# Two attention layers in float32: transposing the softmax maxima of two head groups at once

## The chip, the cores and the metric

The kernel runs on one core of a Trainium2 chip. The metric is device time in microseconds of one launch. The core has a matrix engine (TensorE, PE in the profile, its weight loads PEld), a vector engine (DVE), a scalar engine (ACT), GpSimd (POOL) and a queue for transfers (SP). Matrix products land in PSUM, which has eight banks of 128 x 512 float32.

## What is computed

Two transformer blocks act on x of 4 batches x 512 tokens x 256 channels, all float32. Each has cross attention to a context of 512 tokens (16 heads of 16 channels) and a feed-forward part. The first feed-forward has ternary weights, the second picks one of four experts per token.

```python
x = x + tanh(g_xattn[0]) * xattn0(layernorm(x), ctx, ctx)   # 16 heads, bias -0.1*|q-k|
x = x + tanh(g_ffn[0])   * ffn0(layernorm(x))               # 256 -> 1024 -> 256, ternary
x = x + tanh(g_xattn[1]) * xattn1(layernorm(x), ctx, ctx)   # 16 heads, relu'd q, k, v
x = x + tanh(g_ffn[1])   * ffn1(layernorm(x))               # 4 experts, top 1, then layernorm

# each attention, per batch and head
scores = q @ k.T / 4 (+ bias)
attn   = softmax(scores, axis=-1)
out    = attn @ v
```

## The kernel before

**Groups.** The heads of one batch in one layer are cut into four groups of four heads. Two groups share a chunk of 128 channels (`tt`), one takes the even heads (`e` = 0) and the other the odd (`e` = 1). A head has 16 channels but a slot of 32 rows: in `qs` and `ks` the rows of the other half are zero, and they are spare. There are 2 x 4 x 4 = 32 groups, in the order of `groups`.

**Softmax without a second pass.** A group is worked in two stages. `maxima` (L496) makes scores with queries in the rows, for 128 queries at a time, and DVE takes each row's maximum (L508) into `m_sb`. `shifted` (L559) transposes the four tiles of maxima (L565, PE) into a bank and subtracts that bank from the queries (L567, DVE), which puts the maximum, negated, into a spare row that meets a row of ones in the keys. Layer 0 carries the distance bias in eight more spare rows in the same way. `weights` (L512) then makes scores with keys in the rows from the shifted queries `q2s`, ACT takes the exponential (L523), in layer 0 POOL multiplies the diagonal tile (L526), and `weighted` (L544, PE line L551) multiplies with the values. The last column of the values is one, so the sum comes with it; `divided` (L596) or `divided_blocks` (L577) divides.

**Units.** A unit is one tile of 128 rows of one group; there are 128. `scores(u, vs)` (L531) emits the weights of unit u and the maxima of a later unit side by side: a quad is two products of each kind, in four row tiles of 32 rows, each into a bank of its own. A unit normally has two quads. The four maxima of a unit are drained by DVE, the four weight products by ACT. All PSUM tiles come from one rotation of eight banks, so a product waits until the tile eight places earlier has been read.

**Lead.** Maxima run `LEAD` = 6 units ahead of the weights; four units stand before the first weights, and units 0 and 1 take two units of maxima each:

```python
vs = [u + NT] if u < 0 else [2 * u + NT, 2 * u + NT + 1] if u < LEAD - NT else [u + LEAD]
```

**Slots.** After the scores of unit u, `slot(u)` (L1092) emits everything else: at u % 4 == 0 the values product of the group before, at u % 4 == 2 the transposes of the next group and a division. The rest comes from chains: lists of steps, each with a PE cost and a gap in units to the step before it, and each chain with a start and an end in units. A planner takes the step that is due first while the slot's cost is under `SLOT` = 3.1. Chains hold the layernorms (`prepare`), the key and query projections (`project`, two per batch and layer, one for each chunk), the values, the first feed-forward (`ffn0`), the routing and the first expert tiles. The engines execute in the order in which the program emits. After unit 127 the rest of the expert tiles follows in an order written out by hand.

**Names in the profile.** `pm` is a bank of maxima scores, `psc` of weight scores, `pmT` of transposed maxima, `po` of the values product, `pn` of a transposed output, `pk`, `pq`, `pva` of projections, `ph` and `py_f` of the first feed-forward, `pg` of an expert's hidden layer.

Of the kernel before, what the change touches and what calls it, by code (L numbers as in the profile page):

```python
# [19 lines left out]
P = 128  # L20
# [4 lines left out]
HG = 4  # L25
# [12 lines left out]
T_AHEAD = 4  # L38
LEAD = 6
SLOT = 3.1  # L40

# [7 lines left out]
def flamingo_kernel(ctx: ExitStack, tc: tile.TileContext, t: dict, out: bass.AP):  # L49
# [11 lines left out]
    def bank_psum(name):  # L61
        return ps.tile([P, 512], F32, tag="bank", name=name)
# [71 lines left out]

    kpos = act.tile([P, S], F32, tag="q2", name="kpos")
    nc.gpsimd.iota(
# [4 lines left out]

    def query_key_biases():
        for i in range(2):
            for e in range(2):
                nc.vector.tensor_scalar_mul(bqk[:, i, :, e], qkb[:, i, :], half[:, e : e + 1])
# [17 lines left out]
    )  # L163
    m_sb = [[], []]

    def maxima_places(layer):
        for e in range(2):
            m = act.tile([P, NT, HG, HP], F32, tag=f"m{layer}{e}", name=f"m{layer}{e}", bufs=1)
            nc.gpsimd.memset(m, 0.0)
            if layer == 0:  # L170
                for n in range(NT):
                    r = SPARE[e] + 1 + n
                    nc.gpsimd.memset(m[:, n, :, r : r + 1], -1.0)
                    nc.gpsimd.tensor_copy(
                        m[:, n, :, r + NT : r + NT + 1],
                        tok[:, n : n + 1].unsqueeze(1).to_broadcast([P, HG, 1]),
                    )
            m_sb[layer].append(m)

# [264 lines left out]
    def project(layer, b, tt):  # L444
# [12 lines left out]
        def key_half(pk, e):  # L457
            k = act.tile([P, S], F32, tag="k", name=f"k{nm}{e}", bufs=5)
            h = half[:, e : e + 1]
            if layer == 0:  # L460
                nc.vector.scalar_tensor_tensor(k, pk, h, kext[tt, e], ALU.mult, ALU.add)
            elif e == 0:
                nc.scalar.activation(k, pk, AF.Relu, bias=kone[:, e : e + 1], scale=h)
            else:
                nc.vector.tensor_scalar(k, pk, h, kone[:, e : e + 1], ALU.mult, ALU.max)
            ks[layer, b, tt, e] = k
# [29 lines left out]
    def maxima(v, pair):  # L496

        g = groups[v // NT]
        n = v % NT
        pm = [bank_psum(f"pm{v}{pair}{i}") for i in range(2)]  # L500
        for i in range(2):
            score(pm[i], qs[g], ks[g], 2 * pair + i, n)
        m = m_sb[g[0]][g[3]]
        r = SPARE[g[3]]

        def drain():
            for i in range(2):
                nc.vector.tensor_reduce(m[:, n, 2 * pair + i, r : r + 1], pm[i], AX.X, ALU.max)  # L508

        return drain  # L510
# [47 lines left out]

    def shifted(s):  # L559

        g = groups[s]
        m = m_sb[g[0]][g[3]]
        pm = bank_psum(f"pmT{s}")
        for n in range(NT):
            nc.tensor.transpose(pm[:, ts(n, P)], m[:, n].rearrange("p h w -> p (h w)"), ident)  # L565
        q2s[g] = act.tile([P, S], F32, tag="q2", name=f"q2_{s}")
        nc.vector.tensor_tensor(q2s[g], qs[g], pm, ALU.subtract)  # L567

# [460 lines left out]
    def first_unit(layer, b):  # L1029
        return 4 * NT * (B * layer + b)  # L1030

    ffn = head = None
    ffns = []
    for b in range(B):
        first, rest = ffn0(b)
        end = first_unit(1, b) - 15
        head = chain(first, 4 * NT * (b + 1) + 3, 4 * NT * (b + 1) + 9, head)
        ffn = chain(rest, 0, end, head, ffn)
        ffns.append(ffn)
    for layer in range(2):  # L1040
        for b in range(B):
            u0 = first_unit(layer, b)
            lead, values = prepare(layer, b)
            if (layer, b) == (0, 1):
                *early, early_rows, turn_1 = (job for job, *_ in lead)
                (early_values, *_), later_values = values
                turned_1 = chain([later_values, (turn_1, 0.9, 1)], 1, 4)
                chain(project(layer, b, 0), 5, u0 - LEAD - 2, turned_1)
            elif u0:
                chain(  # L1050
                    [*lead, *project(layer, b, 0)], u0 - 14, u0 - LEAD - 2,
                    ffns[b] if layer else None,
                )
                chain(values, u0 - 8, u0 + 2)
            chain(project(layer, b, 1), max(u0 - 4, 0), u0)
    (totals1, *_), *quant1 = quantize(w1f, "w1")
# [35 lines left out]
    def slot(u):  # L1092
# [4 lines left out]
        if u % NT == 2 and u > 0:  # L1097
            s = u // NT
            if s + 1 < len(groups):
                shifted(s + 1)  # L1100
                used += 0.5
# [24 lines left out]

    maxima_places(0)
    value_places(0)
# [14 lines left out]
    for u in range(-NT, n_units):  # L1143
        if u == 0:
            shifted(0)
            early_values()
            other_constants()
        if u == 4:
            maxima_places(1)
        if u == first_unit(0, B - 1) + 1:  # L1150
            attn_w.append(load_attn(1))
        if u == first_unit(1, 2) + 2:

            wo1 = [const.tile([P, NF // 2, D], F32, tag=f"cT{i}", name=f"wo1{i}") for i in range(2)]
            for i, w in enumerate(wo1):
                rw = t["wo1"][i * FF // 2 : (i + 1) * FF // 2, :]
                nc.sync.dma_start(out=w, in_=rw.rearrange("(c p) f -> p c f", p=P))
        vs = [u + NT] if u < 0 else [2 * u + NT, 2 * u + NT + 1] if u < LEAD - NT else [u + LEAD]
        scores(u, [v for v in vs if v < n_units])
        if u < -NT + 2:  # L1160
# [189 lines left out]
```

## Time and profile before

| | |
|---|---|
| median of 3 runs | 851.79 us (850.83 to 853.1) |
| profiled execution | 852.66 us, its span 851.0 us |
| first score quad of a weight unit | 29.9 us |
| start of the last unit | 699.2 us |
| PE, DVE, ACT, POOL busy | 96%, 66%, 50%, 33% |
| maxima, L508 | 512 instructions, 316.7 us of DVE |
| exponentials, L523 | 512 instructions, 267.0 us of ACT |
| transposes of maxima, L565 | 128 instructions, 21.1 us of PE |
| subtraction, L567 | 32 instructions, 21.6 us of DVE |

In the profile a float32 product counts as two instructions on PE, a transpose as one. "Busy" is the union of the times of a group's instructions, and "idle before" is how long the engine had nothing to do before them, with the engine and line that released it. An instruction on PE is listed when it starts, and its end is modelled. A bank that is not yet free delays the product that wants it.

### The profile page before, as it was taken

How to read it: one execution, taken by the hardware profiler on the slowest of the kernel's cores; microseconds unless marked ns; L12 is line 12 of the kernel's file. 1: busy time of each engine (PE TensorE's matmuls, PEld its weight loads, DVE VectorE, ACT ScalarE, POOL GpSimd, SP SyncE). 2: the span in 40 equal slices, each digit the busy share in tenths (PEclk: the TensorE clock that was granted, in tenths of full speed). 3: DMA queues.
4: the chain of work that ended last, by engine and by line, in shares of the span. 5: the costliest groups of instructions: out<-in, count | busy, mean ns of one | idle time of the engine just before them, and what ended most of it. 6: DMA issues, size and time to landing. Idle time of an engine off the chain costs nothing. (4 is left out here: it accounts for less than half of the span.)

```text
span 851.0 us, 13599 instructions
## 1 busy us (share of the span) xinstructions
PE 818.3 (96%) x5241; PEld 460.4 (54%) x5241; DVE 561.3 (66%) x1218; ACT 422.5 (50%) x886; POOL 277.8 (33%) x446
## 2 busy tenths in 40 slices
PE   6999999999999999999999999999999999999994
PEld 3444444435464346444464445544445567889993
DVE  6868778766856785668746775577786655863343
ACT  2575565653554462556426563357555666224331
POOL 4636455524242433321101120003013224354542
PEclk9999999999999999999999999999999999999998
DMA  9100000000000000000000010001004424536540
GB/s 318 62 1 1 1 1 2 1 1 1 1 13 26 1 1 1 25 2 1 1 2 25 0 50 1 1 1 35 17 13 147 164 70 148 188 108 239 190 152 15
DMA packets 18096, 43.07 MB, mean 51 GB/s; under 512 B 2222, under 2 KB 12208, under 8 KB 15600
## 3 DMA queue, kind: packets, MB, share of 16 engines
q0 software_dynamic: 5488, 28.13, 9.8%
q1 hardware_dynamic: 12128, 13.54, 4.6%
q8 instruction: 41, 0.67, 0.3%
q10 hardware_dynamic: 416, 0.54, 0.2%
q14 instruction: 23, 0.19, 0.1%
HBM read 35.91 MB, written 6.68 MB: 50 GB/s over the span
## 5 line engine op out<-in xcount | busy, mean ns | idle before, releaser
L508 DVE TENSOR_REDUCE m<-pm 128x1 f32<-128x512 f32 x512 | 316.7, 681 | 107.8 <-PE psc L494 105.3
L523 ACT ACTIVATE p<-psc 128x512 f32<-128x512 f32 x512 | 267.0, 602 | 151.2 <-PE psc L494 149.0
L494 PE MATMUL psc<-q,k 32*128 32x512 f32 x1024 | 278.6, 622 | 0.2 <-DVE h L672 0.2
L494 PE MATMUL pm<-k,q 32*128 32x512 f32 x1024 | 262.0, 615 | 1.3 <-ACT q L481 0.9
L526 POOL TENSOR_TENSOR p<-p,dec 128x256 f32<-128x256 f32 x128 | 93.6, 735 | 177.2 <-ACT p L523 177.2
L494 PEld LDWEIGHTS pm<-k,q 32*128 32x128 f32 x1024 | 92.7, 184 | 83.5 <-issue 50.0
L494 PEld LDWEIGHTS psc<-q,k 32*128 32x128 f32 x1024 | 106.4, 183 | 51.7 <-issue 25.7
L551 PE MATMUL po<-p,v 128*32 128x512 f32 x1024 | 116.5, 595 | 1.9 <-DVE m L508 1.9
L551 PEld LDWEIGHTS po<-p,v 128*32 128x32 f32 x1024 | 31.7, 109 | 81.8 <-issue 60.8
L996 PE MATMUL pg<-xs,wg 128*128 128x128 f32 x608 | 72.1, 276 | 0.9 <-DVE m L508 0.9
L996 PEld LDWEIGHTS pg<-xs,wg 128*128 128x128 f32 x608 | 70.4, 192 | 4.4 <-DVE m L508 1.9
L1178 PE MATMUL pyf<-wo,ha 128*128 128x256 f32 x304 | 68.4, 379 | 0.0
L619 POOL TENSOR_TENSOR x<-x,o 128x256 f32<-128x256 f32 x14 | 10.2, 728 | 174.3 <-DVE o L612 131.7
L1009 ACT ACTIVATE ha<-pg,wg 128x128 f32<-128x128 f32 x120 | 34.2, 368 | 62.4 <-PE pg L996 57.0
L1178 PEld LDWEIGHTS pyf<-wo,ha 128*128 128x128 f32 x304 | 56.4, 190 | 7.0
L664 PE MATMUL ph<-xTf,w1q 128*128 128x512 f32 x128 | 60.0, 605 | 0.0
L557 ACT COPY oT<-po 128x512 f32<-128x512 f32 x32 | 18.7, 584 | 77.6 <-PE po L551 77.6
L379 PE MATMUL py_f<-w2q,h 128*128 128x256 f32 x256 | 57.2, 381 | 0.0
L379 PEld LDWEIGHTS py_f<-w2q,h 128*128 128x128 f32 x256 | 48.0, 190 | 9.4 <-DVE m L508 3.0
L451 PE MATMUL pk<-cT,wk 128*128 128x512 f32 x68 | 35.3, 644 | 7.3 <-DMA cT<-in_ctxT_dram 7.3
L664 PEld LDWEIGHTS ph<-xTf,w1q 128*128 128x128 f32 x128 | 22.6, 189 | 30.4 <-issue 18.2
L1182 DVE TENSOR_TENSOR y<-y,pyf 128x256 f32<-128x256 f32 x19 | 8.0, 421 | 43.3 <-PE pyf L1178 39.1
(223 smaller groups left out, 811.2 us busy)
## 6 DMA issues: line engine op xcount, KB each, us to landing
x<-in_x_dram SPq DMA_DIRECT2D x4, 512.0 KB, 7.0
rows_d<-xn_f SPq DMA_DIRECT2D x4, 512.0 KB, 3.0
rows_d<-x SPq DMA_DIRECT2D x4, 512.0 KB, 3.1
cT<-in_ctxT_dram SPq DMA_DIRECT2D x3, 512.0 KB, 9.6
w1q<-in_w_dram SPq DMA_DIRECT2D x1, 1024.0 KB
w2q<-in_w_dram SPq DMA_DIRECT2D x1, 1024.0 KB, 11.3
wo<-in_wo_dram SPq DMA_DIRECT2D x2, 512.0 KB
rows<-in_rows_dram SPq DMA_DIRECT2D x1, 640.0 KB, 9.3
```

The lines of the kernel that those rows point to most:

```text
L379: nc.tensor.matmul(py[:, n, :], lhsT=operand(c, n0 + n), rhs=w[:, c, :], start=(c == 0), stop=(c == chunks - 1),)
L451: nc.tensor.matmul(pp, lhsT=attn_w[layer][w][:, c, ts(tt, P)], rhs=src[:, c, :], start=(c == 0), stop=(c == NC - 1),)
L494: nc.tensor.matmul(out_, lhsT=lhs[r, ts(n, P)], rhs=rhs[r, :], start=True, stop=True)
L508: nc.vector.tensor_reduce(m[:, n, 2 * pair + i, r : r + 1], pm[i], AX.X, ALU.max)
L523: nc.scalar.activation(p[:, i, :], psc[i], AF.Exp, scale=SCALE)
L526: nc.gpsimd.tensor_tensor(d, d, dec.unsqueeze(1).to_broadcast([P, 2, P]), ALU.mult)
L551: nc.tensor.matmul(po[i * HP : (i + 1) * HP, :], lhsT=v_sb[b % 2][0][:, kt, c0 : c0 + HP], rhs=ps_exp[NT * s + kt, i // 2][:, i % 2, :], s ...
L557: nc.scalar.copy(pos[s], po)
L664: nc.tensor.matmul(ph, lhsT=w1q[:, c, ts(f, P)], rhs=st["xT"][:, c, :], start=(c == 0), stop=(c == NC - 1),)
L996: nc.tensor.matmul(ph[:, f, :], lhsT=w[:, c, ts(f2 * NF // 2 + f, P)], rhs=xs[j][:, c, :], start=(c == 0), stop=(c == NC - 1),)
L1009: nc.scalar.activation(ha[:, f, :], (ha if src is None else src)[:, f, :], AF.Gelu, bias=biases[j][:, fa : fa + 1],)
L1178: nc.tensor.matmul(py, lhsT=hs[j, f // 4][:, f % 4, :], rhs=wo1[f // 4][:, f % 4, :], start=(f == 0), stop=(f == NF - 1),)
```

## The change

The first ten groups stay single. From the tenth on the two groups of a chunk, which share their 128 rows, are one turn. Both write their maxima into the same tile: the even group's into row 16 of each head's 32, the odd group's into row 0. One set of four transposes then serves both, and each group takes from it only its own spare rows: the subtraction becomes a multiplication of the bank with a column that is -1 in the group's spare rows and 0 elsewhere, plus the queries. Since the maxima of both groups have to be there, maxima lead the weights by ten units: units 24, 28, 32 and 36 get a second unit of maxima (a third quad). There are two tiles for maxima that alternate between turns, in place of four, and both have the bias rows; POOL clears those rows after the last two turns of layer 0. Keys get one buffer more and shifted queries one. The projections and layernorms of a chunk are due by the unit in which its maxima are emitted, so their chains start and end earlier.

```diff
--- before.py
+++ after.py
@@ -37,6 +37,8 @@
 T_LIST = T_ALL - LISTS[-1][1]
 T_AHEAD = 4
 LEAD = 6
+MORE = (24, 28, 32, 36)
+PAIRED = 10
 SLOT = 3.1
 
 
@@ -132,7 +134,7 @@
 
 
 
-    kpos = act.tile([P, S], F32, tag="q2", name="kpos")
+    kpos = act.tile([P, S], F32, tag="q2", name="kpos", bufs=3)
     nc.gpsimd.iota(
         kpos, pattern=[[1, S]], base=0, channel_multiplier=0, allow_small_or_imprecise_dtypes=True
     )
@@ -140,6 +142,7 @@
     kext = {}
 
     def query_key_biases():
+        nc.vector.tensor_scalar(spare, half, -1.0, None, ALU.add)
         for i in range(2):
             for e in range(2):
                 nc.vector.tensor_scalar_mul(bqk[:, i, :, e], qkb[:, i, :], half[:, e : e + 1])
@@ -161,21 +164,22 @@
     nc.gpsimd.iota(
         tok, pattern=[[-P, NT]], base=0, channel_multiplier=-1, allow_small_or_imprecise_dtypes=True
     )
-    m_sb = [[], []]
-
-    def maxima_places(layer):
-        for e in range(2):
-            m = act.tile([P, NT, HG, HP], F32, tag=f"m{layer}{e}", name=f"m{layer}{e}", bufs=1)
+    m_sb = []
+    spare = const.tile([P, 2], F32, tag="spare", name="spare")
+
+    def maxima_places():
+
+        for i in range(2):
+            m = act.tile([P, NT, HG, HP], F32, tag=f"m{i}", name=f"m{i}", bufs=1)
             nc.gpsimd.memset(m, 0.0)
-            if layer == 0:
-                for n in range(NT):
-                    r = SPARE[e] + 1 + n
-                    nc.gpsimd.memset(m[:, n, :, r : r + 1], -1.0)
-                    nc.gpsimd.tensor_copy(
-                        m[:, n, :, r + NT : r + NT + 1],
-                        tok[:, n : n + 1].unsqueeze(1).to_broadcast([P, HG, 1]),
-                    )
-            m_sb[layer].append(m)
+            for n in range(NT):
+                rows_of = m[:, n].rearrange("p h (e w) -> p (h e) w", e=2)
+                nc.gpsimd.memset(rows_of[:, :, 1 + n : 2 + n], -1.0)
+                nc.gpsimd.tensor_copy(
+                    rows_of[:, :, 1 + NT + n : 2 + NT + n],
+                    tok[:, n : n + 1].unsqueeze(1).to_broadcast([P, 2 * HG, 1]),
+                )
+            m_sb.append(m)
 
     def counting(shape, pattern, base, up, name):
 
@@ -455,7 +459,7 @@
             return pp
 
         def key_half(pk, e):
-            k = act.tile([P, S], F32, tag="k", name=f"k{nm}{e}", bufs=5)
+            k = act.tile([P, S], F32, tag="k", name=f"k{nm}{e}", bufs=6)
             h = half[:, e : e + 1]
             if layer == 0:
                 nc.vector.scalar_tensor_tensor(k, pk, h, kext[tt, e], ALU.mult, ALU.add)
@@ -500,7 +504,7 @@
         pm = [bank_psum(f"pm{v}{pair}{i}") for i in range(2)]
         for i in range(2):
             score(pm[i], qs[g], ks[g], 2 * pair + i, n)
-        m = m_sb[g[0]][g[3]]
+        m = m_sb[turn_of[v // NT] % 2]
         r = SPARE[g[3]]
 
         def drain():
@@ -556,15 +560,30 @@
         pos[s] = act.tile([P, S], F32, tag="oT", name=f"oT{s}")
         nc.scalar.copy(pos[s], po)
 
-    def shifted(s):
-
-        g = groups[s]
-        m = m_sb[g[0]][g[3]]
-        pm = bank_psum(f"pmT{s}")
+
+    turns = [(s,) for s in range(PAIRED)]
+    turns += [(s, s + 1) for s in range(PAIRED, len(groups), 2)]
+    turn_of = {s: i for i, of in enumerate(turns) for s in of}
+
+    def shifted(i):
+
+        m = m_sb[i % 2]
+        pm = bank_psum(f"pmT{i}")
         for n in range(NT):
             nc.tensor.transpose(pm[:, ts(n, P)], m[:, n].rearrange("p h w -> p (h w)"), ident)
-        q2s[g] = act.tile([P, S], F32, tag="q2", name=f"q2_{s}")
-        nc.vector.tensor_tensor(q2s[g], qs[g], pm, ALU.subtract)
+        for s in turns[i]:
+            g = groups[s]
+            q2s[g] = act.tile([P, S], F32, tag="q2", name=f"q2_{s}", bufs=3)
+            nc.vector.scalar_tensor_tensor(
+                q2s[g], pm, spare[:, g[3] : g[3] + 1], qs[g], ALU.mult, ALU.add
+            )
+        if i in last_turns:
+
+            rows_of = m.rearrange("p n h (e w) -> p (n h e) w", e=2)
+            nc.gpsimd.memset(rows_of[:, :, 1 : 1 + 2 * NT], 0.0)
+
+    last_turn = turn_of[len(groups) // 2 - 1]
+    last_turns = (last_turn - 1, last_turn)
 
 
 
@@ -1029,30 +1048,43 @@
     def first_unit(layer, b):
         return 4 * NT * (B * layer + b)
 
+
+    units_of, phase_of = {}, {}
+    for u in range(-NT, n_units):
+        many = 2 if 0 <= u < LEAD - NT or u in MORE else 1
+        units_of[u] = range(len(phase_of), min(len(phase_of) + many, n_units))
+        phase_of |= {v: u for v in units_of[u]}
+    for i, of in enumerate(turns):
+
+        assert phase_of[NT * of[-1] + NT - 1] < NT * of[0] - 2 or i == 0
+        assert i + 2 >= len(turns) or phase_of[NT * turns[i + 2][0]] >= NT * of[0] - 1
+
     ffn = head = None
     ffns = []
     for b in range(B):
         first, rest = ffn0(b)
-        end = first_unit(1, b) - 15
+        end = phase_of[first_unit(1, b)] - 9
         head = chain(first, 4 * NT * (b + 1) + 3, 4 * NT * (b + 1) + 9, head)
         ffn = chain(rest, 0, end, head, ffn)
         ffns.append(ffn)
     for layer in range(2):
         for b in range(B):
             u0 = first_unit(layer, b)
+            at = [phase_of[u0 + 2 * NT * i] for i in range(2)]
             lead, values = prepare(layer, b)
             if (layer, b) == (0, 1):
                 *early, early_rows, turn_1 = (job for job, *_ in lead)
                 (early_values, *_), later_values = values
                 turned_1 = chain([later_values, (turn_1, 0.9, 1)], 1, 4)
-                chain(project(layer, b, 0), 5, u0 - LEAD - 2, turned_1)
+                chain(project(layer, b, 0), 5, at[0] - 2, turned_1)
             elif u0:
                 chain(
-                    [*lead, *project(layer, b, 0)], u0 - 14, u0 - LEAD - 2,
+                    [*lead, *project(layer, b, 0)], at[0] - 8, at[0] - 2,
                     ffns[b] if layer else None,
                 )
                 chain(values, u0 - 8, u0 + 2)
-            chain(project(layer, b, 1), max(u0 - 4, 0), u0)
+            soon = 4 if (layer, b) == (1, B - 1) else 6
+            chain(project(layer, b, 1), max(at[1] - soon, 0), at[1] - 2)
     (totals1, *_), *quant1 = quantize(w1f, "w1")
     (totals2, *_), *quant2 = quantize(w2f, "w2")
     totals = {0: (totals1, 0), 1: (totals1, 2), 2: (totals2, 0), 3: (totals2, 2)}
@@ -1096,8 +1128,8 @@
             used += 3.5
         if u % NT == 2 and u > 0:
             s = u // NT
-            if s + 1 < len(groups):
-                shifted(s + 1)
+            if s + 1 < len(groups) and turns[turn_of[s + 1]][0] == s + 1:
+                shifted(turn_of[s + 1])
                 used += 0.5
             if s > 0 and not by_blocks(s - 1):
                 divided(s - 1)
@@ -1124,7 +1156,7 @@
             if c["steps"]:
                 c["ready"] = u + c["steps"][0][0][2]
 
-    maxima_places(0)
+    maxima_places()
     value_places(0)
     query_key_biases()
     lead, values = prepare(0, 0, nc.vector, lambda: key_rows(0, 0, nc.vector))
@@ -1145,8 +1177,6 @@
             shifted(0)
             early_values()
             other_constants()
-        if u == 4:
-            maxima_places(1)
         if u == first_unit(0, B - 1) + 1:
             attn_w.append(load_attn(1))
         if u == first_unit(1, 2) + 2:
@@ -1155,8 +1185,7 @@
             for i, w in enumerate(wo1):
                 rw = t["wo1"][i * FF // 2 : (i + 1) * FF // 2, :]
                 nc.sync.dma_start(out=w, in_=rw.rearrange("(c p) f -> p c f", p=P))
-        vs = [u + NT] if u < 0 else [2 * u + NT, 2 * u + NT + 1] if u < LEAD - NT else [u + LEAD]
-        scores(u, [v for v in vs if v < n_units])
+        scores(u, units_of[u])
         if u < -NT + 2:
             values[u + NT][0]()
         if u == -NT + 1:
```

## The prediction

> **What bounds the kernel now.** I read the page first: engines, slices, groups.
>
> ```profile
> PE 818.3 (96%) x5241; PEld 460.4 (54%) x5241; DVE 561.3 (66%) x1218; ACT 422.5 (50%) x886; POOL 277.8 (33%) x446
> ...
> PE   6999999999999999999999999999999999999994
> ...
> PEclk9999999999999999999999999999999999999998
> ...
> L508 DVE TENSOR_REDUCE m<-pm 128x1 f32<-128x512 f32 x512 | 316.7, 681 | 107.8 <-PE psc L494 105.3
> ```
>
> PE seems full at a steady clock, so every PE instruction removed should be time gained. The groups with shapes kept apart give the operations of the change, and the timeline, PE alone, a unit without delays:
>
> ```profile
> L567 DVE TENSOR_TENSOR q<-q,pmT 128x512 f32<-128x512 f32 x32 | 21.6, 675 | 1.1 <-PE pmT L565 1.1
> L565 PE MATMUL pmT<-ident,m 128*128 128x128 f32 x128 | 21.1, 286 | 2.5 <-DVE m L508 2.5
> L461 DVE SCALAR_TENSOR_TENSOR k<-pk,cols,kx 128x512 f32<-128x512 f32 x16 | 11.3, 744 | 1.9 <-PE pk L451 1.9
> ...
> 302.41 0.70 PE L494 MATMUL pm<-k,q 32*128 32x512 f32 x2
> 302.42 0.70 PE L494 MATMUL psc<-q,k 32*128 32x512 f32 x2
> ...
> 304.34 1.99 PE L379 MATMUL py_wo<-wo,o 128*128 128x256 f32 x8
> ```
>
> The two score quads of a unit (two maxima and two weight products side by side in four row tiles) take 304.34 - 302.41 = 1.93 us. DVE needs 2.48 for the unit's four maxima. Now the timeline of all engines for a unit behind a projection:
>
> ```profile
> 359.00 0.70 PE L494 MATMUL pm<-k,q 32*128 32x512 f32 x2
> ...
> 359.83 0.75 DVE L487 TENSOR_SCALAR q<-pq,cols 128x512 f32<-128x512 f32 x1 [0.82 <-ACT q L485]
> ...
> 360.49 2.47 DVE L508 TENSOR_REDUCE m<-pm 128x1 f32<-128x512 f32 x4
> 360.63 0.29 PEld L494 LDWEIGHTS psc<-q,k 32*128 32x128 f32 x2 [0.46 <-DVE q L487]
> 360.63 1.12 PE L494 MATMUL psc<-q,k 32*128 32x512 f32 x2
> 361.68 0.66 PE L565 MATMUL pmT<-ident,m 128*128 128x128 f32 x4
> ```
>
> The second quad may start at 359.00 + 0.97 = 359.97. Three of its four products do; the fourth needs the bank that DVE drains until 359.83 + 0.75 = 360.58, runs alone at 360.63, and the unit takes 2.68 in place of 1.93. PE has no idle time in this: the loss is inside its 96%. So the law of this kernel is: **a bank drained after the start of the quad that wants it costs the difference, plus about 0.1** (here 0.61 + 0.1; measured 0.75). I went through the timeline with it, run of quads by run of quads, each against 0.86 us a quad and 0.21 to leave the row tiles: 44.6 us are lost in the whole loop, 14.8 before 124 us, 7.6 from 124 to 353, 20.2 from 353 to 661, 2.0 after.
>
> Here a rule is to be weighed. The row's 96% says that nothing hides in PE. The Trainium skill, "Perfetto Trace Analysis", section "Identifying the Most-Contended Engine", says that matmul occupancy is no good measure, because matmuls are pipelined, and takes the share of weight loads (54% here). By the row the change would give all the PE time that it removes, 5.8 us as worked out below, and 846; by the rule there is lost time inside the busy time that can also grow, up to the +9 at the end of the sum. The timeline above sides with the rule, so both halves of the sum are needed.
>
> **The change, part by part.** The order of the changed kernel's instructions shows that it does what it says: 21 groups of four transposes in place of 32; the ten first groups still single.
>
> 1. *Transposes removed.* From the start of a group to the next PE instruction takes 0.49 to 0.60 in the timeline, 0.53 typically, and in the stage of the pairs PE is the queue that everything stands in. 11 x 0.53 = **-5.8**. Their waits for maxima are not part of it: a group's last maxima are one unit old in both kernels.
>
> 2. *Subtraction.* It becomes a scalar_tensor_tensor. The same operation with PSUM and SBUF inputs has a row, L461: 744 ns against 675. 32 x 0.07 = 2.2 us of DVE; hidden on PE except in the first ten groups, where DVE drains late already: 5 of them in that stage, about +0.3 with the new 128x2 operation ahead of the first statistics (L145's row, a tenth or two).
>
> 3. *Two subtractions in one slot.* This is the main cost. In a pair's slot DVE does 2 x 0.74 = 1.49 where it did 0.68, ahead of everything else the slot leaves to it: division (L605, L607, L612: 0.98 from first to last), half of a layernorm's statistics (two of 0.55), then a hidden tile or a transposed half (0.74, 0.69) whose bank the next quad wants. Two readings are to be weighed again. DVE is busy 66%: by that row a pair costs nothing. The Trainium skill, "TensorEngine Tiling (Array Packing)", section "PSUM Bottleneck", says that tiling speeds up TensorE and not the emptying of PSUM, which may then become the bottleneck: by that rule a pair costs wherever its slot is short. The law above has shown the rule at work in this trace, so I count place by place. Example, unit 62 (groups 16, 17; its slot: transposes, then the eight of pt_f): maxima drained at 3.63 after the unit's start, subtractions at 4.4 and 5.1, statistics 6.2, xTf 6.9. The slot ends at 1.93 + 0.50 (361.68 to 362.18) + 0.96 (to 363.14) = 3.4, and the next unit's second quad, whose last bank is that of xTf, may begin at 4.4, or 4.9 where its first quad is late too. It waits until 6.9: 2.0 to 2.5, I take the lower. Before, the same slot with one subtraction and without the statistics cost 0.19, and the next group's none. So for each pair, quads behind it, after against before (both turns): (10,11) 1.4 / 0.0; (12,13) 0.1 / 0.7; (14,15) 1.3 / 0.1; (16,17) 2.0 / 0.2; (18,19) 1.9 / 0.2; (20,21) 2.6 / 0.2; (22,23) 0.2 / 2.2; (24,25) 2.3 / 3.3; (26,27) 2.7 / 1.9; (28,29) 1.4 / 1.9; (30,31) 0 / 0. After 15.9, before 10.7: **+5.2**.
>
> 4. *Lead of ten.* Units 24, 28, 32 and 36 get a third quad, all maxima; the last ten units have no maxima in place of the last six. The PE time is the same 4 x 0.97, moved. The third quad wants the banks of the first, of which DVE drains the second at 2.39 after the start, while it could start at 1.93: 0.4 each, 1.0 in unit 24 where DVE comes late from w2q. The eight maxima (5.0 us) are covered by the 3.6 us of po behind the quads. **+2.0**. At the end DVE no longer stands before the quads of units 118 to 122, which cost 0.85 and 0.80: **-1.3**; there ACT (2.06 for four exponentials) becomes the longest in two short units, 0.3 of it taken off.
>
> 5. *Projections earlier and split.* Keys and queries are due sooner; the planner puts them into different slots more often (keys at the end of units 22, 26, 34, 82, 98, 106). Either one at a slot's end drains late: layer 0 keys, two DVE operations of 0.74 after the product's end, 0.85; queries, ACT then DVE, 0.75 to 0.9 by the rows before. Joint ones cost that once. I count 12.6 after against 9.7: **+2.9**.
>
> 6. *Other queues.* POOL: start-up has the same 18 small fills and copies, two later fills of 0.5 fall away, two memsets of about 0.5 come after groups 12 and 14, nine units ahead of the maxima that follow; between them stand the 0.73 us products of L526, which po needs, in units of 4 to 9 us: nothing; 0.5 each if that cover were gone. SP: rows, weights and second-layer loads leave in the same units; the expert weights' fetches at 636.8 and 639.4 are used at 645.8 and 665.9, so 5 us less between them is held for the second; the first keeps its distance. **0**. Other slots (pva with two v drains, pt_f alone, divisions alone) come out +0.3, which is nothing at this precision.
>
> Sum: -5.8 + 0.3 + 5.2 + 2.0 - 1.3 + 2.9 + 0.3 = **+3.6**. The profiled execution took 852.66 (span 851.0 and 1.7 around it), so 856.3 on its scale; it lies 0.9 above the median of 851.79, on whose scale I predict **855.3**. Unknown ends: a pair's slot could cost nothing new (DVE at 66%: sum -1.6) or up to 1 us at each of eleven (+9).
>
> **The rivals.** *Faster:* the drains fit after all. The place is the pairs' slots: if DVE's statistics and tiles come late enough for PE in only three of them (as 0.04 to 0.2 behind most single turns might suggest), part 3 falls to zero or below and part 5 to 1: -5.8 + 0.3 + 2.0 - 1.3 + 1.0 = about -4, 848. It decides where the second subtraction's 0.74 fits between the maxima's end (3.63) and the next quad's need; in unit 46 and 86 it does (nothing but an ACT-drained tile comes behind it). Against it: six of the eleven slots have statistics and a DVE drain behind the subtractions. *The same:* half of parts 3 and 5, -5.8 + 0.3 + 2.6 + 2.0 - 1.3 + 1.5 = -0.7, 851. *Much slower:* the thin units 94 to 111 (no filler in 95 and 101) build a DVE queue that runs from pair to pair, as 98 to 100 did before with 3.25 us; four more of these give 862 to 865; a pair relieves the next turn, so I give it little.
>
> **How the numbers follow.** A measurement of this kernel can tell about 0.3% (2.6 us) from no change. Slower begins at 854.3, faster ends at 849.2. As summed 0.52, own range 853 to 860, of which 0.06 lie under 854.3; much slower 0.08; the same 0.18; faster 0.22. So faster 0.22, same 0.18 + 0.06 = 0.24, slower 0.46 + 0.08 = 0.54. The range, 847.5 to 860.5, leaves out about a tenth on each side.
>
> **What would show it.** Right: 84 transposes L573; pairs of DVE subtractions of 740 ns; behind units 38, 62, 70, 78 and 102 a score product alone, 1.4 to 2.7 us after its quad, released by DVE h or xTf; units 118 to 121 shorter by some 5 us, units 24 to 36 longer by 6; PE busy share unchanged. Wrong: behind these units 1.93 us for two quads. Then the saving stands and the time is 848.

## The result: slower, by more than was forecast

The changed kernel takes 863.63 us in the median of four runs (862.7 to 866.52); the kernel before, now with four runs, 851.62. The ratio is 1.0143, 95% interval 1.0127 to 1.0158. A second set of four runs later gave 866.09, ratio 1.0152 (1.0124 to 1.0179). The forecast was 855.3: the direction was right, the size was not. The profiled execution of the changed kernel has a span of 862.3 against 851.0, so 11.3 us are to be explained.

The page of the changed kernel, engines, slices and the group of the maxima (columns as before):

```profile
PE 826.2 (96%) x5197; PEld 457.4 (53%) x5197; DVE 561.7 (65%) x1219; ACT 423.2 (49%) x886; POOL 276.8 (32%) x446
...
PE   6999999999999999999999999999999999899994
...
PEclk9999999999999999999999999999999999999998
...
L512 DVE TENSOR_REDUCE m<-pm 128x1 f32<-128x512 f32 x512 | 316.4, 681 | 96.8 <-PE psc L498 93.9
```

PE issues 44 instructions fewer (5197 for 5241), and yet is "busy" for 7.9 us more: the loss again hides inside its 96%. DVE does the same work and waits 94 us for score products where it waited 105: it stands less and comes later. The groups by shape show that the planned half of the change took place:

```profile
L577 DVE SCALAR_TENSOR_TENSOR q<-pmT,spare,q 128x512 f32<-128x512 f32 x32 | 22.8, 740 | 1.7 <-PE pmT L573 1.7
L573 PE MATMUL pmT<-ident,m 128*128 128x128 f32 x84 | 13.9, 286 | 3.7 <-DVE m L512 3.6
```

The rest is read as the prediction read it: every run of score quads in the timeline against 0.86 us a quad and 0.21 to leave the row tiles. What lies above that is called lateness here.

| units | before | after | difference |
|---|---|---|---|
| up to 16 | 11.4 | 11.5 | +0.1 |
| 17 to 20 | 3.4 | 6.4 | +3.0 |
| 21 to 39 (the ramp: 24, 28, 32, 36) | 3.7 | 9.2 | +5.5 |
| 40 to 127 (pairs) | 26.2 | 32.5 | +6.3 |
| all | 44.6 | 59.5 | +14.9 |

Of the 11.3 us, then: +14.9 lateness, -5.8 transposes, +1.0 in the start-up, +0.8 in the tail (a wait for a gather), and 0.4 not assigned.

The timeline of all engines behind unit 62, the slot that the prediction took as its example (start, length, engine and line, idle time before and its releaser):

```profile
373.76 2.48 DVE L512 TENSOR_REDUCE m<-pm 128x1 f32<-128x512 f32 x4 [0.21 <-PE psc L498]
...
376.17 1.40 DVE L577 SCALAR_TENSOR_TENSOR q<-pmT,spare,q 128x512 f32<-128x512 f32 x2
...
377.48 0.42 DVE L329 BATCH_NORM_STATS2 st_a<-x 128x6 f32<-128x256 f32 x1
...
378.03 0.39 DVE L329 BATCH_NORM_STATS2 st_a<-x 128x6 f32<-128x256 f32 x1
...
378.56 0.66 DVE L376 COPY xTf<-pt_f 128x512 f32<-128x512 f32 x1
...
379.27 0.29 PEld L498 LDWEIGHTS psc<-q,k 32*128 32x128 f32 x2 [1.36 <-DVE xTf L376]
379.27 1.12 PE L498 MATMUL psc<-q,k 32*128 32x512 f32 x2 [0.53 <-DVE xTf L376]
```

The two subtractions stand ahead of two pairs of statistics, these ahead of the eviction of xTf, and a score product waits for that bank until 379.27: unit 63 is late by 2.26 us, where 2.0 was forecast and 0.19 was lost before. PE itself shows 0.53 of it as idle.

The part that was not forecast stands earlier, in unit 20:

```profile
121.35 2.08 ACT L360 ACTIVATE xn_a<-x,off_a,rstd_a 128x256 f32<-128x256 f32 x4 [1.24 <-POOL off_a L347]
...
123.33 1.04 ACT L376 COPY oTT<-pt_o 128x512 f32<-128x512 f32 x2
...
123.95 0.29 PEld L498 LDWEIGHTS psc<-q,k 32*128 32x128 f32 x2 [1.32 <-ACT oTT L376]
123.95 1.12 PE L498 MATMUL psc<-q,k 32*128 32x512 f32 x2 [0.49 <-ACT oTT L376]
```

Here the late engine is ACT. The third batch's layernorm now starts one unit earlier, so its four normalizing activations (2.08 us, behind 1.24 us in which ACT waits for GpSimd) come ahead of the two evictions of the turned outputs, and the second score quad wants one of those banks. In the kernel before, the evictions came first, right behind the products of `pt_o`:

```profile
117.90 1.07 ACT L372 COPY oTT<-pt_o 128x512 f32<-128x512 f32 x2
...
120.71 3.64 PE L551 MATMUL po<-p,v 128*32 128x512 f32 x32
```

Unit 20 loses 2.63 us in place of 0.54.

### The profile page after: what moved, and what is told of

Same layout as the page of the kernel before. It is cut to its first block, busy times and chain, and to the rows that moved or that the text cites. A ratio compares the mean times of both kernels' runs of the same rounds, so it can differ in the third digit from the quotient of the medians.

```text
span 862.3 us, 13520 instructions
## 1 busy us (share of the span) xinstructions
PE 826.2 (96%) x5197; PEld 457.4 (53%) x5197; DVE 561.7 (65%) x1219; ACT 423.2 (49%) x886; POOL 276.8 (32%) x446
## 5 line engine op out<-in xcount | busy, mean ns | idle before, releaser
L498 PE MATMUL psc<-q,k 32*128 32x512 f32 x1024 | 283.1, 624 | 2.7 <-DVE xTf L376 1.1
L498 PEld LDWEIGHTS psc<-q,k 32*128 32x128 f32 x1024 | 104.4, 183 | 59.5 <-issue 24.8
```

The lines of the kernel that those rows point to most:

```text
L498: nc.tensor.matmul(out_, lhsT=lhs[r, ts(n, P)], rhs=rhs[r, :], start=True, stop=True)
```

## Experiments

Theory: the double subtraction costs about what its saved transposes bring, and the loss is the rest of the change, the longer lead: its extra quads stand where DVE is behind, and the earlier preparation is put into bad slots. Rival: the double subtraction is the loss. A second question is what of the 11.3 us is not the change's at all. The kernel before was timed again beside each group of runs, with medians from 851.62 to 853.83, so kernels are compared by their ratios to it.

**Pairs taken apart, lead kept.** The transposes and the subtraction are undone, and the second half's projections start four units ahead again:

```
+    def shifted(s):
+        i = turn_of[s]
...
-        for s in turns[i]:
-            g = groups[s]
+        g = groups[s]
...
-            if s + 1 < len(groups) and turns[turn_of[s + 1]][0] == s + 1:
-                shifted(turn_of[s + 1])
+            if s + 1 < len(groups):
+                shifted(s + 1)
...
-            soon = 4 if (layer, b) == (1, B - 1) else 6
+            soon = 4
```

> The changed kernel, with its lead of ten and its two shared tiles, but from the tenth group on each group is transposed and subtracted by itself, in its own slot, as before (95 sets of transposes in all again), and the second half's projections may start four units ahead instead of six. Theory A, what pairing brings and costs nearly cancels: the eleven extra sets of transposes give back 11 x 0.53 = +5.8 us, and the late drains behind the double subtraction, measured 15.3 us in the slots of groups 10 to 29, go back to about the 10.7 that the same slots lost before; so +1.2 on 863.6, about 865 (862 to 868), and the whole of the loss is the lead, its extra units and the start. Theory B, the double subtraction is what made the kernel slower: about 853 to 857.

Measured: 863.95, ratio 1.0128 (1.0111 to 1.0145); span 861.5. Lateness falls from 59.5 to 54.8: units 40 to 127 are back at 26.4 (before: 26.2), units 17 to 39 stay at 16.4 (before 7.1, after 15.6), where the edit's last line moves projections too. So by this account the pairs are worth -5.8 us of transposes and about +4.7 of late drains: a gain of 1 us, no more. The times do not show so small a gain, since the intervals of the two ratios overlap. Nearly the whole loss is there without any pair. This is theory A.

**The pairs' subtraction off DVE.**

```
+            col = spare[:, g[3] : g[3] + 1]
+            if len(turns[i]) > 1:
+                nc.scalar.activation(q2s[g], pm, AF.Identity, scale=col)
+                nc.gpsimd.tensor_tensor(q2s[g], q2s[g], qs[g], ALU.add)
+                continue
```

> The changed kernel, with the subtraction of paired groups taken off VectorE: ScalarE copies the turned maxima times -1 or the like into the shifted query's place, GpSimd adds the queries. 22 subtractions of 0.74 us leave VectorE. Theory A, the late drains behind the double subtraction cost what was measured in those slots (15.3 us), and only what other VectorE work makes late there stays (some 5): about 863.6 - 10 = 854 (851 to 857). Theory B, the drains are late for another reason (the units' own work on TensorE), or ScalarE's two copies (about 0.7 us each, ahead of the next exponentials) make the weights' banks late instead: 862 to 866.

Measured: 858.11, ratio 1.0056 (1.0039 to 1.0072), span 856.2. Between the two expectations (by its ratio at theory A's upper end): the lateness in the pairs' slots falls from 15.3 to 8.4 us, and unit 63 from 2.26 to 0.95. What stays stands behind statistics and xTf. The drains are late because of DVE's queue, as theory A has it; but the queue is longer than the two subtractions.

**The kernel before, with eleven subtractions issued twice.**

```
+        for _ in range(1 + (s >= 10 and s % 2 == 0)):
-        nc.vector.tensor_tensor(q2s[g], qs[g], pm, ALU.subtract)
+            nc.vector.tensor_tensor(q2s[g], qs[g], pm, ALU.subtract)
```

> The kernel before, with the subtraction of every even group from the tenth on issued twice (eleven more VectorE instructions of 0.675 us, the output unchanged); nothing else differs, TensorE and the lead are as before. The rule of late drains (a bank drained after the start of the quad that wants it costs the difference and 0.1) gives by slot: units 38 0.7, 46 0, 54 0.7, 62 1.4, 70 1.1, 78 0.8, 86 0.7, 94 0, 102 0.7, 110 0.7, 118 0, in all +6.8: 858.4 (856 to 860). The rival, that VectorE's queue takes up 0.7 us anywhere (its busy share is 65%): 851.6 to 852.6.

Measured: 855.45 (13 runs), ratio 1.0037 (1.0024 to 1.0051): half of the expectation, and clear of the rival's. Slot by slot, added lateness (in the unit behind each): unit 39 0.34, 55 0.33, 63 0.72, 71 0.72, 79 0.12, 111 0.72, and nothing in 47, 87, 95 and 103. Where DVE has no slack, the added subtraction moves the next eviction from 0.60 to 1.32 us behind the first one's start (unit 62), and the kernel pays these 0.72 us in full: a further delay of a drain that is late already is passed on one for one. The expectation had read the slack of the other slots too small by 0.3 to 0.7 us.

**The third batch's preparation one unit later.**

```
-                    [*lead, *project(layer, b, 0)], at[0] - 8, at[0] - 2,
+                    [*lead, *project(layer, b, 0)], at[0] - 8 + ((layer, b) == (0, 2)), at[0] - 2,
```

> The changed kernel, with the preparation of the third batch of the first layer started one unit later (its layernorm's statistics in units 18 to 20 as before, not 17 to 20). Theory A: the losses of units 17 to 20 (after 1.77 + 2.01 + 2.63, before 1.12 + 1.71 + 0.54 us) come from that one unit: -2.5 to -3 us, about 861. Theory B: they come from the added work of the first places and stay, or only move by a unit: 863 to 864.

Measured: 863.39, ratio 1.012 (1.0099 to 1.0142), not apart from the changed kernel's; span 861.7. The timeline, however, is plain: units 17 to 20 lose 3.4 us as before the change, and unit 21 starts at 125.48 in place of 128.57.

```profile
119.11 1.07 ACT L376 COPY oTT<-pt_o 128x512 f32<-128x512 f32 x2
...
121.91 3.64 PE L555 MATMUL po<-p,v 128*32 128x512 f32 x32
```

The evictions of oTT now stand ahead of the normalization, and the weighted sums start at 121.91 in place of 125.00. The 3.1 us are given back later in this execution: 0.9 in units 21 and 22, 0.8 in units 113 and 114, and 1.7 in unit 79, in which nothing is later than in the changed kernel. Eight products of the hidden layer, the same in both, in the changed kernel first and then in this one:

```profile
480.00 3.70 PE L683 MATMUL ph<-xTf,w1q 128*128 128x512 f32 x8
```

```profile
477.83 5.40 PE L683 MATMUL ph<-xTf,w1q 128*128 128x512 f32 x8
```

They took 1.7 us longer at a lower granted clock (0.81 and 0.76 from 476 to 484 us, where the changed kernel has 1.00), which is the subject of the last section. The granted clock is the share of its full speed that TensorE was given. So the cause of units 17 to 20 is shown, and its worth in the time is not.

**The ramp later.** The units with two units of maxima at 40 to 52, pairs from the fourteenth group on.

```
-MORE = (24, 28, 32, 36)
-PAIRED = 10
+MORE = (40, 44, 48, 52)
+PAIRED = 14
```

> The changed kernel with the four units that take two units of maxima moved from 24, 28, 32, 36 to 40, 44, 48, 52, and pairing from the fourteenth group on (two pairs fewer, so two sets of transposes more, +1.06 us). Before the change VectorE is busy 72 to 80% of the stretch of units 24 to 36 (140 to 200 us) and 58% at 240 to 260 us, just behind unit 40. Theory A, the ramp is dear because it stands where VectorE is late already: units 21 to 39 fall back from 9.2 us of late drains to about 4, the ramp costs 1 to 2 us at its new place, the two pairs less give back 1.4: about 5 us less than the changed kernel, in its ratio to before about 1.0085 (1.006 to 1.011) in place of 1.0143. Theory B, a unit of three quads costs its 1.3 us anywhere: ratio 1.013 to 1.016.

Measured: 860.35, ratio 1.0087 (1.0067 to 1.0108), as theory A said, but put together otherwise. Units 21 to 39 fall from 9.2 to 5.0 as expected. The ramp's four units lose 5.1 us at 24 to 36 (the same units before: 1.4) and 3.6 at 40 to 52 (before: 1.1), so the new place saves only 1.2 of the ramp's own 3.7. The larger part is that before the ramp the lead is still six: units 17 to 20 have their old preparation and their old 3.4 us. The account is not closed: lateness falls by about 3.2 us in all, and two more sets of transposes take back 1.1, so some 2 of the 4.8 us by which the ratio falls are accounted for. The runs scatter from 857.84 to 865.39, and the profiled one was the slowest.

Why a third quad is dear at unit 28 is seen in the changed kernel:

```profile
168.19 0.81 DVE L487 TENSOR_SCALAR q<-pq,cols,bqk 128x512 f32<-128x512 f32 x1 [1.55 <-ACT q L485]
...
168.92 0.74 DVE L306 SCALAR_TENSOR_TENSOR w2q<-w2q,qthr_w,neg_w 128x512 f32<-128x512 f32 x1
...
169.58 0.68 DVE L376 COPY xTf<-pt_f 128x512 f32<-128x512 f32 x1
...
170.18 3.66 DVE L512 TENSOR_REDUCE m<-pm 128x1 f32<-128x512 f32 x6
...
170.92 1.72 PE L498 MATMUL pm<-k,q 32*128 32x512 f32 x8
```

DVE comes to the unit's first maxima 2.0 us after its start, with two evictions and a quantization step ahead, and then has eight to do.

**Statistics out of the slot of the turn**, in two kernels: in the changed one, with the subtraction off DVE for all groups but the first (the diff is against the kernel with the pairs' subtraction off DVE),

```
-            if len(turns[i]) > 1:
+            if i > 0:
...
-                    [*lead, *project(layer, b, 0)], at[0] - 8, at[0] - 2,
+                    [*lead, *project(layer, b, 0)], at[0] - 6, at[0] - 2,
```

> The changed kernel with the subtraction off VectorE for all groups but the first, and the layernorm of each batch started two units later, so that its first statistics fall in the units of the weighted sums and no longer in the slot in which a group is turned. With the subtraction of pairs alone taken off VectorE, 7.7 us of late drains stayed in the slots of groups 10 to 29, behind statistics of 1.2 us and evictions. Theory A, they come from those statistics: 4 us less than that run, ratio to before about 1.001 (0.998 to 1.003). Theory B, the statistics make others late where they now stand, or the projections pushed together do: ratio 1.004 to 1.008.

and in the one before (against the kernel of the next experiment):

```
-                    [*lead, *project(layer, b, 0)], u0 - 14, u0 - LEAD - 2,
+                    [*lead, *project(layer, b, 0)], u0 - 12, u0 - LEAD - 2,
```

> The kernel of the run before it, and the layernorm of each batch started two units later (statistics in the units of the weighted sums). Theory A, statistics ahead of maxima in the slot of the turn are what is left late: another -1 to -3, ratio 0.991 to 0.996. Theory B, the projections pushed together cost what that saves: ratio within 0.002 of the run before it.

Measured: 859.82, ratio 1.0092 (1.0076 to 1.0109), and 857.06, ratio 1.0058 (1.0041 to 1.0075), against 0.9949 for the same kernel without the shift. Both are misses; the second is worse than either theory, the first at theory B's upper end or above it. Pushed together, the steps of a preparation follow each other so closely that PE stands for them (in the second kernel TensorE waits 2.1 us, until 595.6 us, for an exponential that ACT runs behind a normalization of 2.08), and single units lose 3 us and more (units 85 and 101 in the first). In these kernels, where the preparation starts is worth more than what stands behind a turn.

**The kernel before with the subtraction off DVE**, for all groups but the first:

```
-        nc.vector.tensor_tensor(q2s[g], qs[g], pm, ALU.subtract)
+        if s == 0:
+            nc.vector.tensor_tensor(q2s[g], qs[g], pm, ALU.subtract)
+        else:
+            nc.scalar.activation(q2s[g], pm, AF.Copy, scale=-1.0)
+            nc.gpsimd.tensor_tensor(q2s[g], q2s[g], qs[g], ALU.add)
```

> The kernel before, with the subtraction of all groups but the first taken off VectorE as in that run (ScalarE copies minus the turned maxima, GpSimd adds the queries): 31 x 0.675 us less on VectorE. Doubling eleven of them cost about 2 to 3 us, some 0.25 each. Theory A, VectorE's queue sets the late drains before as well: 31 x 0.25 = -8 at most, with many slots not late, -2 to -5: 848 to 850 (ratio 0.994 to 0.998). Theory B, single subtractions hide, or the copies hold back exponentials: ratio 0.999 to 1.003.

Measured: 847.62, ratio 0.9949 (0.9933 to 0.9966): theory A, and faster than both kernels. Its engines and the two operations that replace 31 subtractions:

```profile
PE 814.0 (96%) x5241; PEld 457.6 (54%) x5241; DVE 548.4 (65%) x1187; ACT 438.3 (52%) x917; POOL 316.3 (37%) x477
```

```profile
L571 POOL TENSOR_TENSOR q<-q,q 128x512 f32<-128x512 f32 x31 | 39.2, 1266 | 168.8 <-ACT q L570 168.8
L570 ACT ACTIVATE q<-pmT 128x512 f32<-128x512 f32 x31 | 19.2, 619 | 0.1
```

The two take 1.89 us where DVE took 0.675, and it pays, since their result is wanted a unit and more later and the engines are free: lateness falls from 44.6 to 39.6.

**The changed kernel once more.**

> The changed kernel once more, unaltered, beside the others, for its losses and its granted clock in a second profile. The late drains repeat (59.5 us, within 0.5). If the low clock of 24 to 32 us is the change's own it is there again (0.6); if it is chance it may be missing (about 1 us less), and a pause such as that of unit 79 (late by 2.7 us) may be followed by a stretch at 0.5 to 0.8 (1.7 us more).

Measured: 866.09, ratio 1.0152 (1.0124 to 1.0179); the profiled run has a span of 862.0. Lateness is 61.5; all slots repeat within 0.1 but units 113 and 114, which lose 2.1 us more (expected within 0.5). Here ACT, not DVE, comes late, in the stage where the gathers run; seven other profiles of these runs show unit 114 at 1.1 to 2.1, three of them of variants of the kernel before, and what sets it stays open. The start-up and the tail are like those of the kernel before: the clock is full, and the last gather is waited for 1.05 us in place of 2.20.

**Both remedies on the changed kernel**: the ramp and the pairs as in the kernel with the later ramp, the subtraction as in the one with the statistics apart, without its shift.

```
+MORE = (40, 44, 48, 52)
+PAIRED = 14
...
+            if i > 0:
+                nc.scalar.activation(q2s[g], pm, AF.Identity, scale=col)
+                nc.gpsimd.tensor_tensor(q2s[g], q2s[g], qs[g], ALU.add)
+                continue
```

> The changed kernel with both remedies: the four units with two units of maxima at 40, 44, 48, 52, pairs from the fourteenth group on, and the subtraction of all groups but the first off VectorE. Nine pairs save 9 x 0.53 = 4.8 us of transposes against the kernel before with the same remedy (847.6). Theory A, the lead and the pairs still make drains late, by some 6 to 7 us more than there (ramp 2, projections and slots 4 to 5): 849 to 851, better than before but not than before with the remedy alone. Theory B, with the double subtraction gone, the saved transposes are a clear gain: 843 to 846.

Measured: 853.01 (20 runs), ratio 0.9988 (0.9981 to 0.9995). Theory A at its upper end: lateness is 49.3, 9.7 above the kernel before with the same remedy, where 6 to 7 were expected (1.6 of it in unit 114); nine sets of transposes bring 4.8. Mended as far as I could, the change is level with the kernel before and 0.4% behind what the same remedy does without it.

**Five subtractions in eight slots of the kernel before.**

```
+        for _ in range(5 if s in range(12, 28, 2) else 1):
-        nc.vector.tensor_tensor(q2s[g], qs[g], pm, ALU.subtract)
+            nc.vector.tensor_tensor(q2s[g], qs[g], pm, ALU.subtract)
```

> The kernel before with the subtraction issued five times in place of once for the groups 12, 14 up to 26 (eight slots, 4 x 0.675 = 2.7 us more of VectorE in each, the output unchanged). By what the doubling cost in each of these slots, the drains get late by 2.0 (unit 46), 2.35, 2.7, 2.7, 2.15, 2.05, 2.0 and 2.0: 18 us, so about 870. Theory A, a pause of TensorE of 2 us or more has a price beyond its own length, since the granted clock is halved for some 3.4 us behind some of them, each 1.7 us: with half of the eight so, +7: 877 (872 to 884), with a wide scatter. Theory B, the price is the lateness alone: 868 to 871, scatter as before.

Measured: 873.95, ratio 1.0245 (1.0226 to 1.0263), so +20.9 on 852. Lateness in the slots grows by 1.70, 2.50, 2.46, 2.33, 2.29, 2.52, 0 and 1.59, less 0.8 behind them: 14.6, short of the expected 18. Units 63, 87 and 103 are longer by another 1.5, 2.4 and 1.7, at a lowered clock (0.67 from 372 to 376 us and 0.80 from 612 to 616 for the first and the last); for unit 87:

```profile
512.00:516.00 4.00, 3.52 (x12) 1.00 (x7) 3.86 (x9) 2.97 (x7) 1.55 (x2) 0.82 0.26 90
516.00:520.00 4.00, 4.00 (x6) 1.40 (x5) 1.48 (x3) 1.09 (x2) 1.49 (x1) 0.50 0.50 172
```

(Stretch and its length, busy time and count of PE, weight loads, DVE, ACT and POOL, then the granted clock, the DMA share and GB/s.) That is 5.6 us on top of the lateness: theory A. The scatter was not wide, 873.37 to 876.48.

**Queries off DVE too**, on the kernel before with the subtraction off DVE:

```
-                if layer == 0 and (e == 0 or b < 2):
+                if layer == 0:
...
-                elif layer == 0:
-                    nc.vector.tensor_scalar(q, pq, h, bqk[:, 0, tt, e : e + 1], ALU.mult, ALU.add)
-                elif e == 0:
-                    nc.scalar.activation(q, pq, AF.Relu, scale=h)
                 else:
-                    nc.vector.tensor_scalar(q, pq, h, 0.0, ALU.mult, ALU.max)
+                    nc.scalar.activation(q, pq, AF.Relu, scale=h)
```

> The kernel before with the subtraction off VectorE for all groups but the first (847.6) and, besides, both evictions of the queries' product on ScalarE (12 of them came from VectorE, 0.74 to 0.81 us each, behind the second half of the keys). Ten runs of scores behind a queries' product still lose 0.8 to 0.9 us each. Theory A, that is VectorE's second eviction ahead of the maxima: -5 to -7, about 842 (ratio to before 0.987 to 0.990). Theory B, the bank of the queries is itself what the scores wait for, or ScalarE's exponentials come late: 846 to 849.

Measured: 845.77, ratio 0.990 (0.9884 to 0.9917), the fastest version here. The ratio is at theory A's end, the slots speak for a mixture: the ten runs of scores behind a queries' product still lose 0.55 to 0.73 us, where they lost 0.82 to 1.12. How much the last step gives is not settled: against the kernel with only the subtraction off DVE it is 1.9 us by the medians and 4.2 by the ratios.

## Why the prediction was right and wrong

- *The reading of the bound* held in every kernel: PE is 96% busy in all of them while the time goes from 845.8 to 874.0, and the share of weight loads, 53% or 54%, tells no more. That time is lost inside the busy share is the timeline's finding, not that of the section cited for it. The busy row's reading, 846, is 17.6 us off: it counts the transposes and nothing that goes the other way.
- *Part 1, transposes:* 84 transposes at 286 ns each, as counted. From the start of a set to the next instruction all sets took 19.8 us and take 13.2, and 0.6 of the difference is one wait behind a set, so the -5.8 stands.
- *Part 3, the pairs*, called the main cost: right. The slots lose 15.3 us (forecast 15.9), unit 63 2.26 (2.0), 71 1.93 (1.9), 79 2.72 (2.6), 95 2.54 (2.3). Of the five units named as signs, four (38, 62, 70, 78) have a score product alone behind them that waits for a hidden tile or xTf; behind 102 the loss is smaller (2.00 for 2.7) and stands behind a division. Against the 10.7 of before that is +4.6 for +5.2, and with the pairs taken apart the account closes at a gain of 1 us. It is the largest single item, but not the cause of the loss: the forecast, too, had it nearly cancel with part 1.
- *Part 2, the first ten groups, was the step that failed.* It put +0.3 on units 0 to 20, for the longer subtraction, and the sum has no other term for them: part 3 counts moved statistics only behind the pairs, and part 5 only keys and queries, so the earlier layernorm of these units was put at nothing. But the lead's due times reach back: the preparation of the third batch starts eight units ahead of the unit in which its first maxima are emitted, which came one unit earlier. Units 17 to 20 lose 3.0 us more. The forecast looked for DVE's queue there; in unit 20, which is 2.1 of the 3.0, it was ACT's, with a normalization ahead of two evictions. Starting the preparation one unit later took the 3.0 us away in the timeline, though in the time this does not stand clear of the noise. This step is the largest error of the sum, but it is 2.8 us of the 7.7 by which the profiled run missed the forecast, not the whole.
- *Part 4, the ramp*, was mis-sized: +2.0 forecast, +3.7 measured (units 24, 28, 32 and 36: 5.1 for 1.4). "Covered by the 3.6 us of po behind the quads" is right for the drains that come after the unit; the ones ahead of it were not counted. At the end, -1.3 was forecast, with 0.3 already taken off; -0.7 came (units 118 and 122 still lose 0.47 and 0.45).
- *Part 5, projections*, with the other slots: +2.9 and +0.3 forecast, +4.3 measured as what is left of the lateness. No run tries this part alone.
- *Not the change's:* +1.0 of the start-up and +0.8 of the tail in the profiled run. The first is the clock (below); the kernel before with doubled subtractions, which issues the same start-up as the kernel before, shows it too. The second is the wait for one gather, 2.20 us there and at most 1.51 in the other profiles.
- *The rivals.* "Much slower" named the time (862 to 865), but its place, a DVE queue through the thin units 94 to 111, gave only 2.8 us of the 14.9 (11.4 to 14.2): the number came out and the reason for it did not. "Faster" fell with part 3.

The forecast's 3.6 and the measured 11.3 differ by part 2 (+2.8), part 4 (+2.2), part 5 and other slots (+1.1), start-up and tail (+1.8), pairs (-0.6) and 0.4 not assigned.

## What to carry to other kernels

When work is moved ahead, list every step whose due time hangs on it, with the engine queues at its new place, before looking at the step that gives the change its name: here the pairs came out as counted and the loss was in the lead that they needed. Where one engine drains the banks of another that is "96% busy", look on the draining engine for work that nobody waits for: with 31 subtractions taken off DVE the kernel before gained 4.4 us, though they take nearly three times as long elsewhere. And ask of a saving on the busy engine what its preparation displaces: here 5.8 us of transposes went, and the lateness grew by 14.9 us.

## What the runs showed of the hardware

A low clock can follow a late drain, which then costs twice. The windows of the kernel with the later ramp, around unit 79, and of the changed kernel at the same place (columns as above):

```profile
476.00:480.00 4.00, 3.46 (x7) 1.09 (x6) 3.93 (x10) 1.60 (x4) 0.73 (x1) 0.78 0.00 0
480.00:484.00 4.00, 4.00 (x6) 1.51 (x5) 1.14 (x5) 0.80 (x2) 2.24 (x7) 0.50 0.00 0
```

```profile
476.00:480.00 4.00, 3.47 (x16) 1.04 (x9) 3.86 (x11) 1.68 (x3) 0.73 (x1) 1.00 0.00 0
480.00:484.00 4.00, 4.00 (x13) 1.75 (x16) 2.55 (x8) 1.28 (x2) 1.39 (x3) 1.00 0.00 0
```

The drains are late by about the same in both, and in one of them the granted clock then falls to a half, and the unit takes 11.63 us for 8.28. In that run units 63, 71 and 79 are longer than the changed kernel's by 1.7, 1.7 and 3.4 us. PE's own idle time ahead of it is only 0.54 us; it has stood for two to three microseconds with one or two of four row tiles at work. The Trainium skill, "TensorE: Matmul & The Clock Gate", section "HAM oscillation — how this bites in real kernels", warns of idle gaps above some 3.4 us: here the clock was halved with no idle time above 0.54 us ahead of it, in some executions and not in others. The eight runs of the changed kernel go with the clock: five with a mean of 0.993 to 0.995 took 862.7 to 864.0, three with 0.988 to 0.989 took 866.5 to 868.3. What decides whether a given pause is followed by a low clock was not tried.

The same happens in the start-up, behind a pause of 1.94 us at the first transposes that every kernel has. Window from 28 to 32 us of the changed kernel, of the kernel before with doubled subtractions, and of the changed kernel the second time:

```profile
28.00:32.00 4.00, 4.00 (x19) 2.61 (x22) 0.55 (x1) 0.59 (x1) 2.95 (x8) 0.61 0.02 6
```

```profile
28.00:32.00 4.00, 4.00 (x18) 2.22 (x20) 0.34 (x2) 0.60 (x2) 2.74 (x4) 0.57 0.02 6
```

```profile
28.00:32.00 4.00, 3.94 (x26) 2.47 (x26) 2.05 (x4) 1.33 (x3) 3.73 (x18) 1.00 0.02 6
```

The clock was 0.61, 0.57 and 1.00: with the same start the low clock comes or stays away. Eight of the fourteen profiles have it, three of them of variants of the kernel before, so this microsecond is not the change's.
